# A graph layer that sorts its edges on the chip: three parts and eight rounds become five parts and ten rounds

## The chip, the core and the metric

The kernel runs on one core of a Trainium2 chip. TensorE (PE; its weight loads are listed as PEld), VectorE (DVE), ScalarE (ACT) and GpSimd (POOL) work side by side, each through its own list of instructions in order; SyncE (SP) here only issues DMAs. The metric is the device time of one execution in microseconds, lower is better. Three runs of the kernel before took 4861.4 to 4865.1 us, median 4864.8.

## What is computed

There are 12,500 nodes with 128 features, and 412,500 edges with 64 features, given in the order of `dst`. The reference, cut to what matters:

```python
h = x @ Wn + bn; q = x @ Wq + bq; k = x @ Wk + bk; v = x @ Wv + bv
eh = edge_attr @ We + be
hmid   = leaky_relu(concat([q[src], k[dst], eh], -1) @ A1 + b1, 0.2)
scores = leaky_relu(hmid @ A2 + b2, 0.2)
w   = softmax(scores.mean(-1), axis=0)              # over all edges
out = segment_sum(w[:, None] * v[dst], src)
y   = layernorm(h + out) * gamma + beta
result = layernorm(x + y)
```

So each edge needs rows of `k` and `v` by `dst`, in whose order the edges stand, and a row of `q` by `src`, in which they are random; and its weighted `v` is added up by `src`.

## The kernel before

*Making records.* The 412,500 edges are 403 groups of 1024. The nodes are split by `src` into 98 blocks of 128. For a group, PE gathers the rows of `k` and `v` with one-hot matrices and adds the edge features (L931, L936); ACT copies the 128 x 260 records out of PSUM (L946); DVE works out where each record belongs, namely the next free place of its block (`onehots`, `masked`, `places`: L851 to L913); POOL writes them there with eight indirect DMAs of 128 records a group (`evacuate`, L958). The place is in a table `rtab` in DRAM, in which each block has `cap` rows. `make(p)` does this for the groups of a part p. It yields six times a group, and between the yields the program puts other work.

*Parts and tables.* `PARTS` cuts the 403 groups into three parts that end at groups 165, 307 and 403. There are two tables (`TABS = 2`), and part p writes to table p % 2. In a block the records of a part fill tiles of 128 rows: `tiles` is how many a part can need (the mean and 4.4 standard deviations), 15, 13 and 9 here, 37 together. The largest sets `cap`.

*Rounds.* A part's tiles are read back in rounds, before the part has ended where that is certain: round r covers tiles t0 to t0 + t of every block, and may begin at a group at which these tiles are full in all blocks (the mean less 4.4 standard deviations); the last round of a part waits for the part's end. The eight rounds have 5, 4, 6 tiles a block, 4, 4, 5, and 4, 5. A *unit* is up to three blocks of a round and at most 15 tiles (`WIDTH`, `BLK`): 33 units in most rounds, 49 in the round of six tiles, 280 together.

*A unit's work* (functions inside `sums_of`): `load` (SP, L1150) brings the tiles, `load_q` the blocks' rows of q. `sources` takes the block-local node numbers, `turn` and `turned` transpose them (PE, ACT), `put` writes them to DRAM from ACT's queue and `spread` (SP, L1204) reads them back onto all partitions. For each slice of four tiles `onehot` (DVE, L1216; one instruction for each block that the slice touches), `hidden` (PE), `sloped` (ACT), `leaky` (DVE, L1253); then `scores`, `above_zero`, `heads`, and for a running softmax `maxima`, `maximum`, `reference` (L1320), `weights`; for each slice `select` (DVE, L1338), `weigh` (ACT, L1352), `add` (PE, L1381); at last `total` (DVE, one L1397 for each block, with the sums of the round before, which `before_it` loaded) and `store`.

*The order.* Everything is put in order by hand. `sums_of` gives each of these functions a step; units follow one another at `every` = 8 steps, 6 or 8 in the last round, and `lags` says how many steps each function stands before or after the unit's own. The last loop of `sorted_path` lays the steps of round r beside the groups from `begun[r]` to `begun[r + 1]`. `begun` is worked out beforehand: a round begins when its tiles are certain and the round before is through, and one that has T tiles in U units is taken to last (T + 2.7 U)/12 groups (`PACE`). Before, the rounds begin at groups 74, 127, 167.1, 227.1, 278, 318.1, 367 and 407.1. What is left when the groups are made is done after them, then the last round with more buffers, then the closing (`closing`): the two norms and the output.

*Fills.* Rows of a block that may stay empty in the first two parts must hold zeros. `fill_piece` (L572) writes them with DMAs on SP: 49 for the first table up to group 72, 49 from `zeros` in DRAM for the second table between groups 74 and 163.

*Checks on the chip.* `certain`, `ended` and `gated` compare the counts of the records with the bounds that the plan assumed; `ended` also makes the mask that the last round of a part uses to leave out rows that no record has reached. In each, `counted` copies the counts (PSUM) to SBUF first.

*Order of DMAs.* A load must come after the scatters whose rows it reads. Where a scatter and a load touch the same table but never the same rows, `declare_no_dep` says so; what isn't declared is waited for.

## Time and profile before

| | before |
|---|---|
| median of 3 runs | 4864.8 us |
| the profiled execution | 4862.1 us |
| its span, first to last instruction | 4860.4 us |
| mean granted TensorE clock | 0.927 |
| busy PE, DVE, ACT, POOL | 4017.1 (83%), 4104.8 (84%), 3110.9 (64%), 3305.1 (68%) us |
| DMA | 1484 MB, mean 305 GB/s |
| first and last scatter begin | 59.0, 4310.6 us |

The profile cuts the span into 40 slices of 121.5 us. Rows of the slices hold one digit for each, the busy share in tenths. In the groups of instructions stand line, engine, operation, what is written and read, shape and count; after the bar the busy time in us and the mean duration of one in ns; after the second bar the idle time just ahead of them and what ended it. A group's busy time counts overlapping instructions once, so it can be less than count times mean. The rows of stretches of time are explained where they stand.

### The profile page before, as it was taken

The page shows a single profiled execution, that of the slowest core. Times are in us where ns is not written, and L with a number is a line of the kernel's source. Part 1 is how long each engine was busy: PE and PEld are TensorE (multiplying, and loading weights), DVE is VectorE, ACT ScalarE, POOL GpSimd, SP SyncE. Part 2 cuts the span into 40 slices and gives each one's busy share as a digit, 9 for nine tenths or more (in the row PEclk, how much of TensorE's full clock was granted, in tenths as well). Part 3 has the DMA queues.
Part 4 walks back from the last instruction along what each step waited for, and adds up shares of the span by engine and source line. Part 5 has one row for each costly group of instructions (what it writes and reads, how often), then busy time and mean ns, then how long its engine had stood idle before and what let it go on. Part 6 is the DMA issues. An engine that isn't in the chain of part 4 may idle for free. (4 is left out here: it accounts for less than half of the span.)

```text
span 4860.4 us, 84339 instructions
## 1 busy us (share of the span) xinstructions
PE 4017.1 (83%) x26346; PEld 3094.3 (64%) x26626; DVE 4104.8 (84%) x8629; ACT 3110.9 (64%) x8211; POOL 3305.1 (68%) x3280
## 2 busy tenths in 40 slices
PE   3655665688888899999998888899899999998997
PEld 2434443566766666777676666666677777666776
DVE  8878886698888888889898888898999998977877
ACT  2332222477776667777776666676777777777886
POOL 4777777777777767777777777777777777731103
PEclk7777776799999999999999999999999999999999
DMA  6778876999999998999998888999999999989964
GB/s 197 265 252 266 269 266 214 335 358 346 350 338 346 363 337 307 310 321 313 322 313 311 301 295 301 322 338 321 329 337 329 340 322 322 339 286 329 324 222 162
DMA packets 608627, 1484.42 MB, mean 305 GB/s; under 512 B 101632, under 2 KB 309395, under 8 KB 606374
## 3 DMA queue, kind: packets, MB, share of 16 engines
q1 hardware_dynamic: 445822, 1049.05, 64.5%
q0 software_dynamic: 154752, 429.39, 23.2%
q8 instruction: 211, 3.46, 0.3%
q14 instruction: 250, 2.05, 0.1%
q10 hardware_dynamic: 7592, 0.48, 0.1%
HBM read 906.61 MB, written 611.06 MB: 312 GB/s over the span
## 5 line engine op out<-in xcount | busy, mean ns | idle before, releaser
L958 POOL DMA_INDIRECT rtab<-rec,idx x3224 | 3220.9, 999 | 1087.4 <-issue 775.9
L946 ACT ACTIVATE rec<-pkv 128x1024 f32<-128x1024 f32 x806 | 821.7, 1019 | 1090.4 <-DMA rtab<-rec,idx 557.5
L1352 ACT ACTIVATE ohw<-ohs,w 128x128 f32<-128x128 bf16 x3626 | 1187.0, 399 | 70.8 <-DVE ohs L1338 39.0
L1381 PE MATMUL psm<-rt,ohw 128*128 128x128 f32 x7252 | 1020.6, 284 | 3.0 <-ACT ohw L1352 2.5
L1381 PEld LDWEIGHTS psm<-rt,ohw 128*128 128x128 f32 x7252 | 934.6, 196 | 82.2 <-ACT ohw L1352 21.4
L936 PE MATMUL pkv<-WeS,eat 128*128 128x256 f32 x3224 | 932.3, 416 | 0.0
L1253 DVE TENSOR_TENSOR hm<-ph,hm 128x512 f32<-128x512 f32 (+1 forms) x932 | 625.0, 671 | 294.9 <-ACT hm L1249 292.8
L931 PE MATMUL pkv<-kvs,ohd 128*128 128x256 bf16 x3224 | 534.5, 293 | 325.9 <-ACT rec L946 319.6
L931 PEld LDWEIGHTS <-ohd 128*128 128x128 bf16 x3224 | 319.4, 105 | 581.0 <-issue 461.9
L936 PEld LDWEIGHTS pkv<-WeS,eat 128*128 128x128 f32 x3224 | 612.5, 211 | 72.2
L1230 PE MATMUL ph<-ident,rt 128*128 128x128 f32 x3626 | 581.3, 282 | 76.8 <-DVE hm L1253 74.8
L1230 PEld LDWEIGHTS ph<-ident,rt 128*128 128x128 f32 x3626 | 415.2, 145 | 304.5 <-issue 145.5
L1216 DVE TENSOR_SCALAR ohT<-rowB,iotaP,power 128x512 bf16<-128x512 uint8 (+3 forms) x1176 | 577.2, 509 | 30.1 <-DMA rowB<-row 30.0
L1249 ACT ACTIVATE hm<-ph 128x512 f32<-128x512 f32 (+1 forms) x932 | 532.6, 571 | 61.8 <-PE ph L1239 25.4
L872 DVE TENSOR_SCALAR ohd<-dstb,node 128x1152 bf16<-128x1152 uint8 x404 | 565.0, 1399 | 6.1 <-PE pkv L931 6.1
L1239 PE MATMUL ph<-ohT,qs 128*128 128x512 bf16 (+2 forms) x2072 | 495.3, 329 | 41.1 <-DVE ohT L1216 24.0
L900 DVE TENSOR_TENSOR ats<-pc,oh 128x792 f32<-128x792 f32 x403 | 392.0, 973 | 27.5 <-PE pc L880 27.5
L1264 PE MATMUL psc<-hm,A2s 128*32 128x512 f32 (+2 forms) x1864 | 370.1, 607 | 44.7 <-DVE hm L1253 33.7
L862 DVE TENSOR_REDUCE few<-oh 128x99 bf16<-128x792 bf16 x403 | 395.1, 980 | 13.9
L1338 DVE TENSOR_TENSOR ohs<-iotaE,sl 128x512 bf16<-128x512 bf16 (+1 forms) x932 | 395.2, 424 | 5.0 <-ACT ohw L1352 4.8
L911 DVE TENSOR_REDUCE pos<-ats 128x8 f32<-128x792 f32 x403 | 390.5, 969 | 1.9
L1329 ACT ACTIVATE w<-S,ref 128x12 f32<-128x12 f32 (+2 forms) x280 | 84.7, 302 | 340.6 <-DVE ref L1320 327.7
(193 smaller groups left out, 4072.3 us busy)
## 6 DMA issues: line engine op xcount, KB each, us to landing
rt<-rtab SPq DMA_DIRECT2D x177, 1560.0 KB
rt<-rtab SPq DMA_DIRECT2D x96, 1950.0 KB
eat<-in_ea SPq DMA_DIRECT2D x201, 512.0 KB
rtab<-rec,idx POOLq DMA_INDIRECT x3224
dstb<-dtab SPq DMA_DIRECT2D x201, 256.0 KB
qs<-qtab SPq DMA_DIRECT2D x224, 192.0 KB
atab<-old SPq DMA_DIRECT2D x224, 192.0 KB
rtab<-zeros SPq DMA_DIRECT2D x49, 780.0 KB
```

What stands on the lines that cost most here:

```text
L872: nc.vector.tensor_scalar(to, row[:, cols], node, None, op0=ALU.is_equal)
L931: nc.tensor.matmul(pk[:, i, h, :], ohd[t], kvs, start=(h == 0), stop=False,)
L936: nc.tensor.matmul(pk[:, i, :, :D], eat[:, (j + i) * P : (j + i + 1) * P], WeS, start=False, stop=True,)
L946: nc.scalar.activation(rec[:, :, :, : 2 * D], pk, AF.Copy)
L958: one_tile = nc.gpsimd.indirect_dma_start(out=rtab[p % TABS][:, :], out_offset=bass.IndirectOffsetOnAxis(ap=idxs[g][:, t : t + 1], axis=0) ...
L1216: nc.vector.tensor_scalar(st["oh"][k][:, (a - t0) * P : (b - t0) * P], st["rowB"][:, a * P : b * P], iotaP, power[:, bs[u] : bs[u] + 1], o ...
L1230: nc.tensor.matmul(ph[:, j * P : (j + 1) * P], st["rt"][:, t0 + j, :D], ident, is_transpose=True, start=(j == 0), stop=False,)
L1239: nc.tensor.matmul(ph[:, cols], st["qs"][:, j0 // t, s, :], oh[:, cols], start=False, stop=(s == 1 and j1 == t0 + n),)
L1249: nc.scalar.activation(hm, state[i]["ph", k][:, : n * P], AF.Copy, scale=SLOPE)
L1253: nc.vector.tensor_tensor(hm, ph[:, : n * P], hm, op=ALU.max)
L1352: nc.scalar.activation(ohw[:, j, :], ohs[:, :, j], AF.Copy, scale=st["w"][:, t0 + j : t0 + j + 1])
L1381: nc.tensor.matmul(st["psS"][:, (1 + u) * P : (2 + u) * P], ohw[:, j, :], st["rt"][:, t0 + j, D : 2 * D], start=(k == 0), stop=(k == t - 1),)
```

## The change

The parts and rounds, the pace that the plan assumes, and what follows from them:

- Five parts end at groups 142, 227, 323, 363 and 403. Their blocks need 13, 8, 9, 4 and 4 tiles, 38 together. Ten rounds of 5, 3, 5 | 3, 5 | 3, 2, 4 | 4 | 4 tiles a block, of 33 units each: 330 units.
- The plan takes a round to last (T + 1.2 U)/11.2 groups. The rounds begin at groups 74, 121.3, 151.1, 198.4, 228.1, 275.4, 305.2, 326.2, 364.8 and 403.3.
- The first, third and fifth part share the first table. The fifth part's records stand nine tiles up in each block (`ABOVE`), above the third's nine tiles. So it may write while the third is still read, and that is declared. `cap` becomes 13 tiles.
- Two mask buffers in place of one. The counts are compared where they are, in PSUM, without the copy.
- A unit of two slices gets the lags of one of three.
- The 49 fills of the second table lie between groups 10 and 134.

```diff
-PARTS = (74, 127, 165), (225, 278, 307), (367, 403)
+PARTS = (74, 113, 142), (189, 227), (274, 301, 323), (363,), (403,)
+ABOVE = (0, 0, 0, 0, 9)
-PACE = 12
+PACE = 11.2
...
-        most = max(self.tiles)
+        most = max(t + above for t, above in zip(self.tiles, ABOVE))
...
-    maskp = pool("mask", 1)
+    maskp = pool("mask", 2)
...
+                    if ABOVE[p]:
+                        for k in range(len(PARTS[p - TABS])):
+                            tc.declare_no_dep(
+                                one_tile, group=f"loads{p - TABS}.{k}", reason="other tiles"
+                            )
...
-            runf = counted()
-            pcs.pop(p)
+            run = pcs.pop(p)
             low, over = lims.pop(p)
-            worst(low, runf, low, 2 + 2 * r)
-            worst(runf, over, over, 3 + 2 * r)
+            worst(low, run, low, 2 + 2 * r)
+            worst(run, over, over, 3 + 2 * r)
...
-            o = lags(p, nk)
+            o = lags(p, max(nk, 3))
...
+            t0 += ABOVE[p]
...
+            if p + TABS < NP and ABOVE[p + TABS]:
+                for k in range(len(PARTS[p + TABS])):
+                    tc.declare_no_dep(rows_in, group=f"rows{p + TABS}.{k}", reason="other tiles")
...
-        free_at += sum(len(bs) * t + 2.7 for q, bs, _ in units if q == p) / PACE
+        free_at += sum(len(bs) * t + 1.2 for q, bs, _ in units if q == p) / PACE
...
-            1, n1, n2 - 12, zeros
+            1, 60, n2 - 48, zeros
...
-        fills = fills[::-1]
+        fills = sorted(fills, key=lambda piece: piece[0])[::-1]
```

20 lines of the change are left out of this document (10 added, 10 removed).

## The prediction

> **What bounds the kernel now.** First the page's slices, to see which resource is full and where.
>
> ```profile
> DMA  6778876999999998999998888999999999989964
> GB/s 197 265 252 266 269 266 214 335 358 346 350 338 346 363 337 307 310 321 313 322 313 311 301 295 301 322 338 321 329 337 329 340 322 322 339 286 329 324 222 162
> q0 software_dynamic: 154752, 429.39, 23.2%
> ```
>
> Then the scatter's own line, and the loads that read the table back, each with its first and last start:
>
> ```profile
> L958 POOL DMA_INDIRECT rtab<-rec,idx x3224: 954/960/2788, 59.0 to 4310.6; - x190
> L1150 SPq DMA_DIRECT2D rt<-rtab x280: 370/416/1373, 864.9 to 4672.1; - x140
> ```
>
> So there are three stages: making alone until 864, making and reading together until 4311, and a tail of 549.4 us to the end of the span. Last, the busy times by stretch (length, then PE, PEld, DVE, ACT and POOL busy with instructions, clock, DMA share, GB/s). The windows of the rounds reach from a round's first running reference (L1320) to its last: rounds 0, 1, 4, 5; then the busiest slice, the whole middle stage, and the tail up to round 7 and through it.
>
> ```profile
> 927.00:1449.00 522.00, 456.71 (x3283) 366.84 (x3311) 467.37 (x944) 382.37 (x1001) 398.38 (x405) 0.98 1.00 349
> 1462.00:1901.00 439.00, 390.27 (x2547) 295.79 (x2578) 369.44 (x780) 298.04 (x827) 315.46 (x320) 0.95 0.96 338
> 3056.00:3483.00 427.00, 387.79 (x2578) 293.66 (x2608) 374.59 (x788) 299.36 (x831) 323.68 (x330) 0.97 0.93 326
> 3502.00:3981.00 479.00, 437.61 (x3180) 355.74 (x3209) 451.62 (x970) 380.85 (x1013) 367.06 (x368) 0.97 0.95 333
> 3767.00:3889.00 122.00, 113.22 (x829) 92.52 (x836) 116.63 (x249) 96.95 (x258) 93.66 (x94) 0.97 0.97 341
> 864.00:4311.00 3447.00, 3070.60 (x20919) 2375.40 (x21162) 3035.19 (x6313) 2432.60 (x6608) 2599.51 (x2632) 0.97 0.94 328
> 4311.00:4398.00 87.00, 76.03 (x499) 54.63 (x506) 55.09 (x152) 54.66 (x169) 4.74 (x3) 0.95 0.86 299
> 4398.00:4717.00 319.00, 295.31 (x2345) 238.35 (x2373) 251.61 (x680) 279.82 (x823) 25.12 (x12) 1.00 0.84 288
> ```
>
> Eight scatters are one group. Round 0: 405 scatters, 50.6 groups, 10.31 us a group; round 1: 40 groups, **10.98**; round 4: 41.25, 10.35; round 5: 46, 10.41. POOL issues at nearly the same pace although DVE's share goes from 0.84 (round 1) to 0.94 (round 5), so the middle stage goes at POOL's pace, about 10.35. Only round 1 is slower; there the fills of the second table share the DMA engines. In the busiest slice POOL still does 94 scatters, with DVE at 116.63/122 = 0.956. The tail has no POOL work: PE is busy 295.31 of 319.
>
> The profiled execution took 4862.1 us (span 4860.4 and 1.7 around it); the median of the runs shown, 4864.8, lies 2.7 above. The sum is made against 4862.
>
> **The change, part by part.** Its plan follows from the sizes (412,500 edges, 98 blocks, 403 groups). Before, eight rounds of 5, 4, 6 | 4, 4, 5 | 4, 5 tiles a block. After, ten of 5, 3, 5 | 3, 5 | 3, 2, 4 | 4 | 4: 38 tiles, and 33 units in each round, 330 in place of 280.
>
> *Tail.* Before, the last round had 15 tiles a unit; now it has 12. Before it was to begin at 407.1 groups, 4.1 after the last, so 4.1/40.1 of round 6's 264 steps, 27 steps or 3.4 units, were left: at 319/32 = 9.97 us a unit, 33 us of the 87. After, 403.3: two steps, 2 us. So 87 becomes 56. A unit of 15 keeps PE busy 295.31/32 = 9.23 us. What doesn't shrink with tiles is mainly the sum over heads, eight instructions of 72.8/576 = 0.126:
>
> ```profile
> L1290 PE MATMUL psm<-headsum,z 128*128 128x4 f32 x576 | 72.8, 244 | 18.8 <-ACT ohw L1352 6.1 <-DVE old L1397 4.2 <-ACT rec L946 2.7
> ```
>
> The other 8.2 over 15 tiles gives 6.6 for 12, with the heads 7.6; at PE's share of 0.926 that is 8.2 us a unit. That is the low end, 9.97 (nothing shrinks) the high one. I take 8.7, near the low end, because the turn and the maximum don't shrink either. 32 × 8.7 = 278, and from 4717 to the end of the span, 143, stays: 56 + 278 + 143 = 477, **72 saved** (88 to 31).
>
> *Middle stage.* The work taken out of the tail, and one more tile a block, must fit beside the same 329 groups. Units a group rise: 33 over 29.8 groups is 1.107 with 3 tiles (three rounds), 33/21 = 1.571 with 2, 33/38.5 = 0.857 with 4 (two rounds), 33/47.3 = 0.698 with 5 (three rounds). DVE's prices (groups of DVE's instructions, in 3524 to 3889; the last two rows are of the whole run):
>
> ```profile
> L872 DVE TENSOR_SCALAR ohd<-dstb,node 128x1152 bf16<-128x1152 uint8 x35 | 49.1, 1403 | 0.0
> L900 DVE TENSOR_TENSOR ats<-pc,oh 128x792 f32<-128x792 f32 x36 | 35.0, 972 | 0.5 <-PE pc L880 0.5
> L911 DVE TENSOR_REDUCE pos<-ats 128x8 f32<-128x792 f32 x36 | 34.8, 968 | 0.1
> L862 DVE TENSOR_REDUCE few<-oh 128x99 bf16<-128x792 bf16 x35 | 34.3, 981 | 1.2
> L851 DVE TENSOR_TENSOR oh<-blk,iotaE 128x792 bf16<-128x792 bf16 x35 | 19.7, 562 | 0.0
> L913 DVE SCALAR_TENSOR_TENSOR idx<-pos,twin 128x8 int32<-128x8 f32 x36 | 6.0, 167 | 1.2
> L1253 DVE TENSOR_TENSOR hm<-ph,hm 128x512 f32<-128x512 f32 x73 | 49.7, 681 | 8.8 <-ACT hm L1249 8.7
> L1253 DVE TENSOR_TENSOR hm<-ph,hm 128x384 f32<-128x384 f32 x24 | 13.2, 552 | 3.7 <-ACT hm L1249 3.7
> L1216 DVE TENSOR_SCALAR ohT<-rowB,iotaP,power 128x512 bf16<-128x512 uint8 x25 | 14.0, 559 | 0.1
> L1216 DVE TENSOR_SCALAR ohT<-rowB,iotaP,power 128x384 bf16<-128x384 uint8 x48 | 23.5, 490 | 0.0
> L1216 DVE TENSOR_SCALAR ohT<-rowB,iotaP,power 128x256 bf16<-128x256 uint8 x48 | 19.2, 442 | 0.0
> L1216 DVE TENSOR_SCALAR ohT<-rowB,iotaP,power 128x128 bf16<-128x128 uint8 x24 | 8.4, 348 | 0.0
> L1338 DVE TENSOR_TENSOR ohs<-iotaE,sl 128x512 bf16<-128x512 bf16 x72 | 29.8, 415 | 0.0
> L1338 DVE TENSOR_TENSOR ohs<-iotaE,sl 128x384 bf16<-128x384 bf16 x24 | 10.5, 438 | 0.0
> L1397 DVE SCALAR_TENSOR_TENSOR old<-old,by,psm 128x128 f32<-128x128 f32 x72 | 20.5, 339 | 1.5 <-PE psm L1381 1.5
> L1319 DVE TENSOR_REDUCE m<-psm 128x1 f32<-128x128 f32 x24 | 6.8, 282 | 0.0
> L1305 DVE TENSOR_REDUCE mx<-S 128x1 f32<-128x15 f32 x24 | 4.1, 169 | 0.8
> L1253 DVE TENSOR_TENSOR hm<-ph,hm 128x256 f32<-128x256 f32 x3 | 1.2, 417 | 0.0
> L1338 DVE TENSOR_TENSOR ohs<-iotaE,sl 128x256 bf16<-128x256 bf16 x3 | 0.9, 286 | 0.0
> ```
>
> A group: 1.403 + 0.972 + 0.968 + 0.981 + 0.562 + 0.167 = 5.05. Whatever its tiles, a unit has three `old` (1.02), `m` (0.28) and four short ones such as `mx` (0.67): 1.97. Slices hold four tiles, and L1216 splits a slice at each block. 5 tiles: hm 2.60, ohT 2.77, ohs 1.68, in all 9.02. 4 tiles: 2.04, 1.68, 1.25, in all 6.93. 3 tiles, slices of 4, 4 and 1: hm 1.64, ohT 0.490 + 0.348 + 2 × 0.442 + 0.348 = 2.07, ohs 1.03, in all 6.71 (the 128-wide hm and ohs are not in the trace: 0.28 and 0.2 by the steps between the widths). 2 tiles: 1.10, 1.33, 0.70, in all 5.10. A unit of nine tiles costs DVE nearly what one of twelve does. Durations overlap: round 5 adds up to 32.5 × 9.02 + 46 × 5.05 = 525 against 451.62 busy, and round 4 to 434 against 374.59: 0.86 of the sum. Busy DVE a group after:
>
> - 5 tiles 0.86 × (0.698 × 9.02 + 5.05) = 9.76; 4 tiles 9.45; **3 tiles 10.73; 2 tiles 11.23**.
>
> The first two lie under POOL's pace, the last two above it. How full DVE can get isn't shown: at least 0.956, where POOL hadn't slowed, at most 1. I take 0.98: 10.95 and 11.46 us a group.
>
> Sum by planned groups (98 blocks of t tiles and 1.2 for each of 33 units, over 11.2; together 329): round 0, 47.3 × 10.33 = 489 (round 0's pace); two rounds of 5, 94.6 × 10.41 = 985 (round 5's); three of 3, 89.4 × 10.95 = 979; the one of 2, 21 × 11.46 = 241; two of 4, 77 × 10.35 = 797 (round 4's): 3491. At the end of a part PE begins the next counts only when DVE has read the old ones (the one wait of this kind in 1560 to 1860):
>
> ```profile
> PEld pc L800 <- DVE run L995: 3.7, 1, 3.7
> ```
>
> Two more ends, 3 us each: 3497, that is **50 more** than 3447. With DVE at 1 it is 25 less, at 0.956 30 more. PE's share, 3070.60/3447 = 0.89 now, rises too; up to the tail's 0.926 I count no stall of its own.
>
> Short slices pay more than their share: from 512 to 256 columns `hm` falls by 264 ns, from 681 to 417, so some 153 ns are left at no columns. [...]
>
> *Fills.* The second table's 49 moves leave groups 74 to 163 and go to 10 to 134. Until 74 they meet DMA shares of 0.6 to 0.8, as the page's row shows: nothing, up to 10 if SP's queue is held. What round 1 lost (10.98 against 10.41, over 40 groups 23 us) isn't in my sum, so this gain is counted.
>
> *Latency in the round of 2.* Steps per unit stay at eight, while a unit takes only 11.46 × 21/33 = 7.3 us. In eight steps the numbers of a unit go from ACT to DRAM and back to all partitions; SP waits for the first half alone:
>
> ```profile
> SPq L1204 <- DMA row<-slT: 1918.3, 277, 13.0
> ```
>
> 1918.3/277 = 6.9 us. Behind it on SP stand the loads of `old`, `rt`, `qs`, `kvs` and `eat`, all needed later. If the trip needs a tail unit's 9.97 us, 33 units lose 88 us; at best nothing. I take nothing, since DVE has other units' work ahead of it, and keep 88 for the range.
>
> *The rest* is nothing: the counts read from PSUM without a copy save some ten DVE instructions of 99 columns; the second mask buffer costs memory alone, and lets a mask be made while the one before is read; the fifth part's place above the third's lets scatters go on while round 7 still reads, as the pauses at part ends need.
>
> Sum: 4862 + 50 − 72 = **4840**.
>
> **Rivals.** (a) *POOL keeps its pace* everywhere: DVE overlaps more, and 329 × 10.35 = 3405, or up to 3462. Time 4748 to 4805. For it: no slowing at 0.956. Against it: 10.73 and 11.23 of pure DVE work.
>
> (b) *Gain and loss cancel*: the middle grows by 62 to 82, 4852 to 4872.
>
> (c) *Slower: the DMA engines become the bound.*
>
> ```profile
> rt<-rtab SPq DMA_DIRECT2D x177, 1560.0 KB
> eat<-in_ea SPq DMA_DIRECT2D x201, 512.0 KB
> dstb<-dtab SPq DMA_DIRECT2D x201, 256.0 KB
> kvs<-kvtab SPq DMA_DIRECT2D x403, 64.0 KB
> qs<-qtab SPq DMA_DIRECT2D x224, 192.0 KB
> ```
>
> A group moves 256 + 128 + 64 and eight scatters of 130 (429.39 MB/3224): 1488 KB. A unit moves 130 a tile, three times 192 and 16 a tile: 2766, 2328, 1890, 1452 KB for 5, 4, 3, 2 tiles. Round 4 checks: 139 MB in 427 us, 326 GB/s. After, the stage moves 1193 MB in place of 328 × 3.447 = 1131. Break-even is 1193/(3447 + 72) = 339 GB/s: round 0 held 349 at full pace, round 1 lost pace at 338. If all 329 groups go at round 1's 10.98, the stage takes 3612, and the time is 4862 + 165 − 72 = 4955.
>
> (d) *The tail doesn't shrink with its tiles*, being bound by its chain (9.97): 31 saved, 4881; or the row trip of round 6 costs its 88: 4928.
>
> (e) *The short instructions' latency doesn't overlap.* Without the 0.86, 3 tiles take 12.5 us a group and 2 tiles 13.1; those rounds alone add 171: 5011. Against it: round 5 would take 525/46 = 11.4 and took 10.41. [...]
>
> **How the numbers follow.** Chances: forecast (4805 to 4852) 0.36; (a) 0.18; (b) 0.14; (c) 0.24; (d) 0.07; (e) 0.01. About 0.2% is what a measurement can tell from no change. Faster 0.54, same 0.14, slower 0.32. The range leaves out the best half of (a) and the worst of (c): 4775 to 4915; the forecast's own is 4805 to 4852.
>
> **What would show it.** Right: the last scatter near 4361 and 477 from there to the end, units of the last round 8.7 us apart, 10.9 us a group in the rounds of 3 with DVE over 0.96. Wrong: a last scatter at 4311 or before (a), or past 4400 with DVE waiting for `rt` or `rowB` (c, d); last units still 10 us apart (d).

## The result and the profile after

| | before | after |
|---|---|---|
| median of 4 runs | 4863.7 us | 5182.2 us |
| lowest and highest | 4861.4, 4865.1 | 5174.9, 5196.9 |
| the profiled execution, its span | 4862.1, 4860.4 us | 5181.2, 5179.4 us |
| busy DVE | 4104.8 us (84%) | 4310.3 us (83%) |
| last scatter begins, first rows loaded | 4310.6, 864.9 us | 4712.5, 873.1 us |

The changed kernel takes 1.0659 times as long, with a 95% interval of 1.0635 to 1.0683. That is 6.6% slower, and outside the predicted range of 4775 to 4915. First the lines of the scatters and of the loads of the changed kernel: kind and count, shortest, median and longest duration in ns, first and last start.

```profile
L963 POOL DMA_INDIRECT rtab<-rec,idx x3224: 954/960/2823, 59.3 to 4712.5; - x190
L1155 SPq DMA_DIRECT2D rt<-rtab x330: 370/408/1491, 873.1 to 4995.9; - x165
```

The first stage ends 8 us later than before. The middle stage, from the first load to the last scatter, takes 3840 us in place of 3447, **393 more** (predicted: 50). The tail takes 5179.4 - 4712.5 = 467 us in place of 549, **82 less** (predicted: 72). So the whole miss lies in the middle.

Next the busy times by stretch of the changed kernel, with the columns of the same view of the kernel before: stretch and length, then PE, PEld, DVE, ACT and POOL busy with instructions, clock, DMA share, GB/s. The first nine are rounds 0 to 8 from their first reference (L1328) to their last, round 8 cut at the last scatter; then the rest of round 8, round 9, and the middle stage.

```profile
938.00:1413.00 475.00, 434.49 (x3201) 349.10 (x3201) 435.43 (x903) 367.01 (x976) 352.17 (x359) 0.98 0.98 343
1425.00:1814.00 389.00, 331.93 (x2283) 256.25 (x2281) 325.33 (x796) 260.10 (x732) 243.07 (x245) 0.96 0.87 291
1833.00:2305.00 472.00, 430.75 (x3167) 346.53 (x3168) 436.97 (x957) 374.01 (x1003) 347.29 (x351) 0.98 0.93 325
2317.00:2708.00 391.00, 334.27 (x2281) 258.27 (x2281) 326.08 (x798) 259.81 (x733) 243.92 (x246) 0.95 0.85 284
2725.00:3197.00 472.00, 430.59 (x3162) 349.16 (x3164) 438.61 (x956) 373.81 (x1002) 344.42 (x351) 0.97 0.94 326
3209.00:3583.00 374.00, 326.22 (x2224) 253.10 (x2223) 309.61 (x776) 250.82 (x716) 221.47 (x223) 0.95 0.85 276
3592.00:3920.00 328.00, 282.00 (x1665) 204.28 (x1664) 239.93 (x619) 205.20 (x571) 177.70 (x181) 0.90 0.79 258
3932.00:4347.00 415.00, 381.70 (x2554) 286.44 (x2553) 363.95 (x772) 293.76 (x822) 293.92 (x301) 0.98 0.92 319
4360.00:4713.00 353.00, 322.85 (x2200) 244.79 (x2199) 307.48 (x661) 253.76 (x715) 253.74 (x258) 0.99 0.92 319
4713.00:4768.00 55.00, 48.56 (x304) 33.06 (x303) 31.97 (x87) 33.02 (x103) 2.56 (x2) 0.94 0.81 288
4768.00:5041.00 273.00, 266.35 (x1840) 196.59 (x1838) 200.19 (x530) 212.71 (x664) 27.89 (x13) 0.99 0.83 292
873.00:4713.00 3840.00, 3411.82 (x23575) 2649.14 (x23575) 3317.27 (x7501) 2725.56 (x7479) 2596.57 (x2631) 0.96 0.90 309
```

A round has 33 units, and so 32 intervals between its first and last reference; POOL's count over eight gives its groups. That makes this table (DVE's share is its busy time over the length):

| round, tiles | us between units | groups between units | us a group | DVE's share | predicted us a group |
|---|---|---|---|---|---|
| 0, 5 tiles | 14.84 | 1.40 | 10.58 | 0.92 | 10.33 |
| 2 and 4, 5 tiles | 14.75 | 1.37 | 10.76 | 0.93 | 10.41 |
| 7, 4 tiles | 12.97 | 1.18 | 11.03 | 0.88 | 10.35 |
| 1 and 3, 3 tiles | 12.16, 12.22 | 0.96 | 12.70, 12.72 | 0.84, 0.83 | 10.95 |
| 5, 3 tiles | 11.69 | 0.87 | 13.42 | 0.83 | 10.95 |
| 6, 2 tiles | 10.25 | 0.71 | 14.50 | 0.73 | 11.46 |

Two things stand out. In the rounds of three and two tiles, which were to be bound by DVE at 0.98, DVE is busy 0.84 to 0.73 of the time, and no other column is full in its place: PE is at 0.85 to 0.87, and the DMA share falls to 0.87 to 0.79. And a unit doesn't get shorter in proportion to its tiles. From 15 tiles and 1.37 groups to 6 tiles and 0.71 groups it goes from 14.75 to 10.25 us. A straight line through these two is 5.5 us for a unit and 6.8 us for a group beside it; the rounds between lie within 0.5 us of that line (0.96 groups: 12.0 by the line, 12.2 measured).

The line describes these rounds; it can't tell what a unit costs by itself, because tiles and groups fall together in it. Two things on record hold one of them fixed. In the run with the plan's old pace (`e1_old_pace`, below) the rounds of three and two have the same tiles and 0.05 to 0.09 groups more to a unit; summed over the four rounds, a unit takes 0.81 us more for 0.27 groups, some 3 us a group. By that a unit of nine tiles has about 9 us of its own (12.2 less 0.96 groups at 3), an estimate from single runs. And units of the last round, which has an order of its own and no groups, take 8.5 us with 12 tiles here and took 10.0 with 15 before. So the part that doesn't shrink with the tiles, called the toll below, is large, but its size isn't settled. More rounds of fewer tiles are more units, and every unit pays it.

Where the 343 us beyond the forecast lie: the rounds of three and two tiles took 1482 us for 895 scatters, 111.9 groups; at the predicted 10.95 and 11.46 they would have taken 1237, so **245** are theirs. The rounds of five and four took 2187 us for 202.5 groups, 2100 by the forecast: **87**. The other 11 are in the turns from round to round.

Last the waits, first in a round of three tiles after (2317 to 2708), then in a round of four before (3056 to 3483, 427 us): who waited for whom, us in total, times, longest (`issue`: idle time for which the profile shows no cause).

```profile
ACT w L1337 <- DVE ref L1328: 70.6, 28, 5.2
POOL rtab L963 <- issue: 56.9, 186, 0.6
DVE hm L1261 <- ACT hm L1257: 56.0, 36, 3.4
POOL rtab L963 <- ACT rec L952: 46.1, 23, 4.9
```

```profile
ACT w L1329 <- DVE ref L1320: 50.6, 23, 4.5
ACT rec L946 <- PE pkv L936: 45.4, 17, 4.7
DVE hm L1253 <- ACT hm L1249: 32.4, 30, 3.6
ACT rec L946 <- DMA rtab<-rec,idx: 12.7, 8, 3.8
```

Before, ACT at times waited for the DMAs of scatters before it wrote records (12.7 us); POOL's side was the later one. After, it is POOL that waits for ACT's records (46.1 us). DVE's whole idle time in this round is 391 - 326 = 65 us, and 56 of them are one wait: the leaky maximum (L1261) for ACT's slopes (L1257), 1.7 us a unit. ACT in its turn stands 70.6 us, 2.2 us a unit, before the weights (L1337), for the reference (L1328), which DVE makes once PE has turned the maxima. Slopes and records stand behind the weights in ACT's list, and they can be late with them: ACT stood idle for 5.16 us and began the weights at 2461.13; the slopes behind them began at 2463.83, and at 2464.32 the copy of records whose product (L941) PE had ended at 2459.10.

### The profile page after: what moved, and what is told of

Same layout as the page of the kernel before. It is cut to its first block, busy times and chain, and to the rows that moved or that the text cites. A ratio compares the mean times of both kernels' runs of the same rounds, so it can differ in the third digit from the quotient of the medians.

```text
span 5179.4 us, 90440 instructions
## 1 busy us (share of the span) xinstructions
PE 4299.8 (83%) x28288; PEld 3302.9 (64%) x28288; DVE 4310.3 (83%) x9597; ACT 3312.5 (64%) x8854; POOL 3309.2 (64%) x3280
## 5 line engine op out<-in xcount | busy, mean ns | idle before, releaser
L951 ACT ACTIVATE rec<-pkv 128x1024 f32<-128x1024 f32 x806 | 821.3, 1019 | 1053.7 <-PE pkv L941 514.1
L1360 ACT ACTIVATE ohw<-ohs,w 128x128 f32<-128x128 bf16 x3724 | 1228.7, 399 | 79.6 <-DVE ohs L1346 32.8
L1389 PE MATMUL psm<-rt,ohw 128*128 128x128 f32 x7448 | 1082.9, 287 | 11.3 <-ACT ohw L1360 10.3
L1389 PEld LDWEIGHTS psm<-rt,ohw 128*128 128x128 f32 x7448 | 977.7, 196 | 105.4 <-ACT ohw L1360 33.5
L1261 DVE TENSOR_TENSOR hm<-ph,hm 128x512 f32<-128x512 f32 (+3 forms) x1046 | 655.7, 627 | 403.3 <-ACT hm L1257 401.8
L941 PE MATMUL pkv<-WeS,eat 128*128 128x256 f32 x3224 | 941.8, 420 | 0.0
L936 PE MATMUL pkv<-kvs,ohd 128*128 128x256 bf16 x3224 | 541.4, 296 | 289.8 <-ACT rec L951 285.6
L1238 PE MATMUL ph<-ident,rt 128*128 128x128 f32 x3724 | 614.8, 283 | 88.5 <-DVE hm L1261 87.2
L1224 DVE TENSOR_SCALAR ohT<-rowB,iotaP,power 128x256 bf16<-128x256 uint8 (+3 forms) x1469 | 657.1, 472 | 36.7 <-DMA rowB<-row 36.5
L941 PEld LDWEIGHTS pkv<-WeS,eat 128*128 128x128 f32 x3224 | 618.5, 213 | 74.5
L936 PEld LDWEIGHTS <-ohd 128*128 128x128 bf16 x3224 | 317.9, 105 | 526.5 <-issue 416.7
L1247 PE MATMUL ph<-ohT,qs 128*128 128x256 bf16 (+3 forms) x2938 | 586.8, 304 | 43.7 <-DVE ohT L1224 43.4
L1238 PEld LDWEIGHTS ph<-ident,rt 128*128 128x128 f32 x3724 | 426.2, 145 | 295.0 <-issue 129.2
L1257 ACT ACTIVATE hm<-ph 128x512 f32<-128x512 f32 (+3 forms) x1046 | 561.2, 537 | 64.0 <-PE ph L1247 22.6
L877 DVE TENSOR_SCALAR ohd<-dstb,node 128x1152 bf16<-128x1152 uint8 x404 | 565.0, 1399 | 6.1 <-PE pkv L936 6.1
L1272 PE MATMUL psc<-hm,A2s 128*32 128x512 f32 (+3 forms) x2092 | 440.4, 587 | 47.4 <-DVE hm L1261 41.0
L1346 DVE TENSOR_TENSOR ohs<-iotaE,sl 128x512 bf16<-128x512 bf16 (+3 forms) x1046 | 436.0, 417 | 0.8 <-ACT ohw L1360 0.8
L1337 ACT ACTIVATE w<-S,ref 128x15 f32<-128x15 f32 (+3 forms) x330 | 99.8, 302 | 526.2 <-DVE ref L1328 516.8
L867 DVE TENSOR_REDUCE few<-oh 128x99 bf16<-128x792 bf16 x403 | 395.1, 980 | 13.9
```

Source lines behind the costliest of these rows:

```text
L877: nc.vector.tensor_scalar(to, row[:, cols], node, None, op0=ALU.is_equal)
L936: nc.tensor.matmul(pk[:, i, h, :], ohd[t], kvs, start=(h == 0), stop=False,)
L941: nc.tensor.matmul(pk[:, i, :, :D], eat[:, (j + i) * P : (j + i + 1) * P], WeS, start=False, stop=True,)
L951: nc.scalar.activation(rec[:, :, :, : 2 * D], pk, AF.Copy)
L1224: nc.vector.tensor_scalar(st["oh"][k][:, (a - t0) * P : (b - t0) * P], st["rowB"][:, a * P : b * P], iotaP, power[:, bs[u] : bs[u] + 1], o ...
L1238: nc.tensor.matmul(ph[:, j * P : (j + 1) * P], st["rt"][:, t0 + j, :D], ident, is_transpose=True, start=(j == 0), stop=False,)
```

## The experiments

Two readings were tested first. *The unit's toll is DVE's*: DVE's own work and its waits in series set the pace. *It is something else*: PE, whose share was 0.85 to 0.92 in the rounds, the DMA engines, the plan's tighter pace, or the fills. Each experiment was executed once, unless an interval is given; the four runs of the changed kernel spread over 22 us, so smaller differences say nothing. The kernel before, run beside them, took 4854 to 4872 us. The changed kernel's 5181.2 us is what the differences are taken from.

### The plan's pace, the fills, and the width of units

The old pace in the changed kernel (`e1_old_pace`):

```diff
-PACE = 11.2
+PACE = 12
-        free_at += sum(len(bs) * t + 1.2 for q, bs, _ in units if q == p) / PACE
+        free_at += sum(len(bs) * t + 2.7 for q, bs, _ in units if q == p) / PACE
```

> The changed kernel with the plan's old pace ((T + 2.7 U)/12 groups a round): rounds of 3 lie over 31.9 groups instead of 29.8, of 2 over 23.8 instead of 21, and 13 units of round 8 are left when the groups are made. Theory W (a unit costs VectorE its work and its waits wherever it lies): the middle stage loses 13 units, the tail gains them; 5170 to 5240 in all. Rival O (the rounds are only pressed too tight, and spread out they go at POOL's pace again): last scatter 4330 to 4420, 4870 to 4980 in all.

Measured: 5165.9 us, 15 less, no more than the spread, and just below the 5170 to 5240 of the first case. The last scatter came 133 us sooner (4579.7), and the tail took 117 us more: what the middle gained by taking fewer units came back in the tail, so the plan isn't pressed too tight; the work is too long.

The new place of the fills alone, in the kernel before (`e5_before_fills`):

```diff
-            1, n1, n2 - 12, zeros
+            1, 60, n2 - 48, zeros
-        fills = fills[::-1]
+        fills = sorted(fills, key=lambda piece: piece[0])[::-1]
```

> The kernel before with the new place of the second table's fills alone (groups 10 to 163 in this plan instead of 74 to 163). The prediction's step: round 1 goes at 10.4 instead of 10.98 us a group, 15 to 23 us less: 4840 to 4850. Rival (the fills cost the first stage as much as they cost round 1): 4855 to 4870.

Measured: 4856.8 us, ratio 0.9994 (0.9981 to 1.0008). The move does nothing that can be seen. It isn't the round without fills, though: in this plan the fills reach to group 157, so 7 of them still begin in round 1, where 15 did; that round took 437 us in place of 439.

Smaller units in the kernel before: with a width of 12, its rounds of five tiles have 49 units of ten tiles in place of 33 of fifteen (`e13_before_width12`). Parts, tables, fills and pace stay.

```diff
-WIDTH = 15
+WIDTH = 12
-    TM = max(min(BLK, WIDTH // t) * t for *_, t in plan.rounds)
+    TM = 15
```

> The kernel before with units of at most 12 tiles: rounds 0, 5 and 7 (5 tiles a block) get 49 units of ten tiles instead of 33 of fifteen; nothing else. Theory W (each unit has its own waits and fixed work): rounds 0 and 5 rise from 10.33 and 10.45 to 11 to 12 us a group, 5000 to 5080 in all. Theory B (only VectorE's busy time counts, up to a share of 0.98): its work is 9.4 to 9.8 us a group, under POOL's pace; only the tail's 16 more units count: 4870 to 4910.

Measured: 5098.1 us, 5% slower. Its rounds 0 and 5 by stretch:

```profile
909.00:1513.00 604.00, 531.37 (x3557) 405.42 (x3603) 497.37 (x1093) 416.20 (x1126) 424.46 (x432) 0.96 0.94 319
3553.00:4148.00 595.00, 524.50 (x3527) 401.81 (x3574) 495.71 (x1129) 424.88 (x1166) 407.43 (x414) 0.97 0.85 288
```

48 intervals: 12.6 and 12.4 us a unit, 11.2 and 11.5 us a group, with DVE at 0.82 and 0.83. In the kernel before, the same tiles in units of fifteen went at 10.3 and 10.4. The tiles, the edges and the DMA bytes (1484 MB) are the same; only the number of units rose. So the toll isn't a matter of the new parts. Of the 236 us, 135 had come by the last scatter (4445.4 in place of 4310.6); the other 101 are the tail, whose last round has 16 units more.

### What one wait is worth

Without the reference in the weights, in the changed kernel and in the one before (`e3_no_ref`, `e6_before_no_ref`). The running maximum is still computed, but the exponentials take a constant instead of it.

```diff
-                st["w"][:, :nt], st.pop("S")[:, :nt], AF.Exp, bias=ref[:, u : u + 1],
-                scale=1.0 / H,
+                st["w"][:, :nt], st.pop("S")[:, :nt], AF.Exp, bias=eps,
+                scale=1e-6,
```

> The changed kernel with the weights of a unit taken without the running reference (the exponential gets a constant bias and a scale of 1e-6): what is left out is that each unit's weights are relative to the maximum so far, so ScalarE no longer waits for VectorE's reference (516.8 us of waits in the changed kernel); every instruction stays. Theory A (a unit costs some 6 us of the interleaved program whatever its tiles, because ScalarE, in order, stands still until the chain maximum, TensorE, reference is through, and the record copies and the slopes behind it come late): units of the rounds of 3 come 10 to 11 us apart instead of 12.2, those of 2 under 9.5 instead of 10.3, the last scatter 200 to 350 us earlier, 4850 to 4980 us in all. Theory B (VectorE's own work is the limit, only at a share of 0.83 and not 0.98): the waits move elsewhere, 5140 to 5190.

> The kernel before with the same part left out (the weights' reference). Both theories: its middle stage goes at POOL's pace, so at most the slow stretches go (to 329 x 10.35 = 3405, 42 us) and a little of the tail: 4800 to 4865.

Measured: 5059.7 us, 122 less; in the kernel before 4838.6, 22 less than its neighbour. The first lies between its two cases, the second in the range that was expected. The round of three and the round of two of the changed kernel without the reference:

```profile
2292.00:2658.00 366.00, 323.51 (x2292) 257.93 (x2290) 325.19 (x800) 260.95 (x736) 244.78 (x246) 0.96 0.90 304
3510.00:3813.00 303.00, 265.75 (x1653) 197.38 (x1653) 241.80 (x624) 204.75 (x573) 174.28 (x180) 0.92 0.85 281
```

The round of three goes from 391 to 366 us with the same 325 us of DVE work, so DVE's share rises to 0.89. The last scatter came 125 us sooner, so all of it is the middle's. The wait for the reference is part of the toll, a third of what the middle lost, and no more.

The leaky maximum one step later (`e11_leaky_later`), so that ACT has more time for the slopes:

```diff
-        f = L + 4 + 3 * e
+        f = L + 5 + 3 * e
-            leaky=2, scores=L + 1, above=L + 2 + e, heads=L + 3 + 2 * e, maxima=f,
+            leaky=3, scores=L + 2, above=L + 3 + e, heads=L + 4 + 2 * e, maxima=f,
```

> The changed kernel with VectorE's part of the slope (leaky) one step later in the order of every round but the last, and all behind it one step later too. Theory W (VectorE's in-order stream is the loop: its own work and, in each unit, 1.75 to 2.5 us in which it stands still for ScalarE's slope, so short rounds pay that more often per group): most of the 401.8 us of these waits go, units of the rounds of 3 come 10.8 to 11.4 us apart instead of 12.2, 4950 to 5080 in all. Rival (the waits only show where the engines' chains meet; another wait takes their place): 5150 to 5220.

Measured: 5180.1 us, no change. Rows of the waits over the whole run, of the changed kernel and then of this one:

```profile
ACT w L1337 <- DVE ref L1328: 516.8, 253, 6.9
...
DVE hm L1261 <- ACT hm L1257: 401.8, 329, 3.6
...
POOL rtab L963 <- ACT rec L952: 241.1, 141, 5.0
```

```profile
ACT hm L1257 <- PE ph L1247: 489.4, 281, 6.1
...
POOL rtab L963 <- ACT rec L952: 311.1, 158, 5.6
...
DVE hm L1261 <- ACT hm L1257: 151.2, 139, 3.5
...
ACT w L1337 <- DVE ref L1328: 98.8, 79, 3.3
```

The move did what it was to do: DVE's wait for the slopes fell to 151 us, and ACT's for the reference to 99. But ACT now waits 489 us for PE's hidden layer (L1247), 22.6 in the changed kernel. The rival was right for the total: a wait that is moved turned up on the next engine. By rounds it was not nothing: the second round of three took 371 us in place of 391, but the round of two 340 in place of 328, and the first of four 425 in place of 415.

The weights and all behind them two steps later, for units of up to three slices (`e16_weights_later`, and the same in the kernel before, `e17_before_weights_later`):

```diff
+        x = 2 if nk <= 3 else 0
-            reference=f + 2 + e, weights=f + 3 + e, old=f - 1, lowered=f + 6 + e,
+            reference=f + 2 + e, weights=f + 3 + e + x, old=f - 1, lowered=f + 6 + e + x,
...
```

> The changed kernel with a unit's weights, and what follows from them, two steps later in the order, for units of up to three slices outside the last round; the result is the same. If ScalarE's wait for the reference holds up the slopes and copies behind it (leaving the reference out gave 122 us), most of that comes without leaving anything out: 5040 to 5090. Rival (as with the later slope, another wait takes its place): 5150 to 5200.

> The kernel before with the same move. Its middle stage goes at POOL's pace in most rounds; leaving the reference out gave 22 us there. If the wait is what counts: 4835 to 4852. Rival: 4855 to 4870.

Measured: 5119.2 us, 62 less, half of what leaving the reference out gave and short of the 5040 to 5090 expected; in the kernel before 4887.5, ratio 1.0034 (1.0021 to 1.0048), slightly slower, and above both of its cases.

### What each engine's work is worth

Work was added to DVE (the count of the one-hots, L867, twice) and to ACT (the first copy of the records, L951, twice), in every group, and work was left out: the sums of the second and third block of a unit on DVE (L1405), one of the two products of q on PE (L1247).

```diff
+                nc.vector.tensor_reduce(
+                    few[g], oh.rearrange("p h b t -> p b h t"), AX.XY, ALU.add
+                )
```

```diff
+            if j == 0:
+                nc.scalar.activation(rec[:, :, :, : 2 * D], pk, AF.Copy)
```

```diff
-            for u in range(m):
+            for u in range(1):
```

```diff
-                for s in range(2):
+                for s in range(1):
```

> The changed kernel with one more VectorE instruction per group: the count L867 (0.98 us) done twice with the same result. Theory B: in the rounds of 3, 2 and 4 tiles (about 190 groups) each group takes 0.9 us more, and those of 5 a little: 5330 to 5400. Theory A: VectorE stands idle for 17% there, most of it goes into the idle time: 5190 to 5260.

> The changed kernel with one more ScalarE instruction per group: the first of the two record copies L951 (1.02 us) done twice with the same result. Theory A: ScalarE's order is the loop, so the rounds of 3, 2 and 4 tiles take 0.9 us more a group: 5330 to 5400. Theory B: ScalarE is busy for only 66% there, so nothing comes of it: 5180 to 5220.

> The changed kernel with one instead of up to three L1405 per unit: the other blocks of a unit keep the sums of the round before, their new sums are left out. VectorE has 0.5 to 0.7 us less to do per unit, at the end of a unit's chain. If VectorE's stream is the bound of the short rounds, a unit comes 0.5 to 0.7 us sooner (rounds of 3: 11.5 to 11.7 instead of 12.2), 5000 to 5070 in all. If the bound is TensorE's stream: 5140 to 5185.

> The changed kernel with one instead of two products of the one-hot rows with q (L1247): the lower half of q's bits is left out. TensorE has some 0.8 us less to do per unit (in the rounds of 3 L1247 is busy 52.4 us for 32 units). If TensorE's stream is the bound: 4950 to 5030. If VectorE's is: 5130 to 5185.

Measured, in this order: 5521.5, 5275.9, 5112.3 and 5212.3 us. 0.98 us more for DVE in each of 329 groups are 322 us, and cost 340: the full price and a little more, above both cases. (The expectation of `e18` below spread this cost over all 403 groups, hence its 0.84 a group.) 1.02 us more for ACT are 336 and cost 95, between the cases. DVE's two sums of 0.34 us less in 297 units are 202 us; DVE's busy time in the middle fell by 124 (3317.27 to 3193.64), less than that in part because durations overlap (all 882 such sums of the changed kernel, 341 ns each, add up to 301 us and keep DVE busy for 252.6), and 69 came back, again between the cases. PE's product less gave nothing: the time is 31 us longer, more than the spread, though PE was busy 90 us less in the middle (3411.82 to 3322.10); the granted clock of the run was 0.903 in place of 0.920. The round of three with the doubled count, then with the sums left out:

```profile
2434.00:2860.00 426.00, 351.26 (x2280) 270.54 (x2280) 357.96 (x832) 260.94 (x733) 246.38 (x249) 0.90 0.81 263
```

```profile
2302.00:2681.00 379.00, 331.47 (x2274) 260.92 (x2274) 309.55 (x731) 259.93 (x732) 243.12 (x244) 0.95 0.88 290
```

35 us longer than 391, for 31 counts that keep DVE busy 32 us more. DVE's idle time stays: 426 - 358 = 68 us, 65 before. Work and waits stand in series on DVE, so its stream is on the path though DVE isn't full. Two reservations: the granted clock fell from 0.95 to 0.90 in this round, and PE was busy 17 us longer with the same work; and the count is one that PE's sums wait for (L885: 98.4 us in 40 waits in the changed kernel), so another DVE instruction need not cost as much. Taking work away gives back less: 69 of 124 us. So something close behind takes over.

To measure this from the other side, two thirds of the one-hot columns of dst were left out (L877; the records then hold the rows of k and v of wrong nodes), in the changed kernel and in the one before, and combined with the earlier edits (`e18` to `e21`). Two last ones leave the product of the edge features out of the records (L941), alone and with both others (`e22`, `e23`).

```diff
-            for r in (slice(0, 3),) if g + 1 < G or first else (slice(0, 2), slice(2, 3)):
+            for r in (slice(0, 1),):
...
-                wide[:, t // 3, t % 3 * P : t % 3 * P + P] for t in range(first, first + GT)
+                wide[:, 0, t % 3 * P : t % 3 * P + P] for t in range(first, first + GT)
```

```diff
-                        start=(h == 0), stop=False,
+                        start=(h == 0), stop=(h == 1),
...
-            for i in range(2):
-                nc.tensor.matmul(
-                    pk[:, i, :, :D], eat[:, (j + i) * P : (j + i + 1) * P], WeS,
-                    start=False, stop=True,
-                )
```

> The changed kernel with a third of the one-hot columns of dst made for each group (384 of 1152; the rows of k and v of the other tiles come from wrong nodes). DVE's instruction goes from about 1.40 to about 0.5 us, 0.9 us a group less. It is the mirror of the doubled count (0.98 us more cost 0.84 us a group). If DVE's own stream, work and waits in series, sets the pace of the changed kernel, 0.84/0.98 of it is saved in 329 groups: about 250 us, 4900 to 4960, and a unit of 3 tiles takes about 11.4 us. If DVE and the other engines bind each other, so that less work on DVE only lengthens its waits, a third is saved, as with the sums left out: 70 to 110 us, 5070 to 5115.

> The kernel before with the same part left out. If its making and reading goes at a pace set elsewhere than on DVE, as the prediction read it, the time stays within 30 us: 4830 to 4870. If DVE's stream sets the pace there too, 0.75 us a group less, about 250 us: 4600 to 4660.

> The changed kernel with both left out: two thirds of the dst one-hot columns, and the reference in the weights (which alone took 122 us off). If DVE's work and its waits stand in series, the savings add up: about 370 us, 4780 to 4850. If one of them binds only while the other is there, the time is little below the lower of the two alone: 4880 to 4940 when the first alone gives 4930, 5020 to 5060 when it gives 5090.

> The changed kernel without the reference in the weights and with the leaky maximum one step later. Without the reference DVE still waited 196 us for ACT's slopes. If that wait is now what the time hangs on, moving it takes most of it away: 4880 to 4960. If the units' chain only shifts its waits, as it did with the leaky maximum moved alone, the time stays at 5040 to 5070.

> The changed kernel with the product of the edge features left out of the records (eight matmuls a group; they kept PE busy 67.0 us in the round of 391 us, 2.2 us a group). If PE's stream sets the pace, up to POOL's 10.4 us a group is reached: 4790 to 4900. If DVE's stream, work and waits in series, sets it, PE being in front of it only in short waits: 5120 to 5190. If the engines bind each other, a part of the 2.2 us a group comes back: 4920 to 5110, and DVE's share in the rounds of three rises from 0.83.

> The changed kernel with three parts left out: edge features in the records, the reference in the weights, two thirds of the dst one-hot columns (the last two alone gave 4963). If what was left in the rounds of three and two tiles (11.4 and 13.4 us a group, PE at 0.91 and 0.89) was PE, they come to 10.4 to 10.8 and 11.5 to 12 and the time to 4830 to 4890. If it was a chain of steps that no engine's work lengthens, they stay: 4930 to 4965.

| left out of the changed kernel | us | against 5181.2 |
|---|---|---|
| dst columns (`e18`) | 5040.1 | -141 |
| reference in the weights (`e3`) | 5059.7 | -122 |
| both (`e20`) | 4962.8 | -218 |
| reference; leaky later (`e21`) | 5137.3 | -44 |
| edge product (`e22`) | 5126.0 | -55 |
| edge product, reference, dst columns (`e23`) | 4885.9 | -295 |

Against what was expected: `e18` and `e20` lie between their cases, `e21` above both of its cases, `e22` in the range for DVE's stream. The time of `e23` lies in the range that was set for PE as the bound (4830 to 4890), though its rounds of three and two are slower than that case had them.

The kernel before without the dst columns (`e19`) took 4834.8 us, 34 less than beside it. DVE's instruction fell from 1403 to 410 ns (the expectation's 0.5 us was a little high), so 327 us of DVE work went: the changed kernel gives back 0.43 of it, the one before 0.1. (DVE's busy time in the middle of the changed kernel fell by 307 us, to 3010.22; 141 are 0.46 of that, and the 69 of 124 were 0.56.) Two rounds of the kernel before without the columns (its rounds 4 and 5, of four and five tiles):

```profile
3040.00:3451.00 411.00, 382.52 (x2597) 290.82 (x2596) 336.27 (x784) 297.64 (x828) 314.68 (x317) 0.98 0.96 334
3470.00:3956.00 486.00, 443.91 (x3211) 359.05 (x3210) 409.73 (x969) 381.47 (x1015) 372.71 (x372) 0.97 0.94 329
```

411/39.6 = 10.4 and 486/46.5 = 10.5 us a group, as with all the DVE work (10.35 and 10.41), with DVE's share down to 0.82 and 0.84. That is a floor which doesn't depend on DVE's work. Nor is it the DMA engines, whose share is 0.96 and 0.94 here: round 3 of the kernel before, of four tiles with 1.48 groups to a unit, goes at 489/47.5 = 10.3 as well, with DVE at 0.84, PE at 0.85 and a DMA share of 0.87:

```profile
2553.00:3042.00 489.00, 413.75 (x2711) 314.43 (x2742) 410.99 (x832) 315.96 (x862) 373.49 (x380) 0.96 0.87 303
```

The changed kernel reaches the floor too once it is relieved. A round of three, the round of two and a round of five, without dst columns (`e18`), then without the reference as well (`e20`), then without the edge product too (`e23`):

```profile
2259.00:2632.00 373.00, 334.19 (x2281) 261.71 (x2281) 295.80 (x798) 259.88 (x734) 245.68 (x249) 0.95 0.90 300
3476.00:3793.00 317.00, 278.05 (x1668) 205.29 (x1667) 220.06 (x623) 204.82 (x571) 176.28 (x180) 0.91 0.82 267
2648.00:3097.00 449.00, 420.96 (x3173) 343.77 (x3173) 398.02 (x960) 373.48 (x1004) 343.86 (x346) 1.00 0.96 341
```

```profile
2244.00:2600.00 356.00, 324.56 (x2279) 256.42 (x2279) 295.76 (x796) 259.03 (x734) 248.42 (x250) 0.96 0.93 315
3422.00:3720.00 298.00, 264.01 (x1658) 196.90 (x1655) 218.43 (x620) 204.00 (x574) 175.62 (x179) 0.93 0.86 284
2615.00:3064.00 449.00, 421.46 (x3170) 344.75 (x3170) 398.01 (x956) 372.27 (x1005) 343.53 (x347) 0.99 0.97 340
```

```profile
2224.00:2569.00 345.00, 287.15 (x2044) 219.00 (x2044) 294.86 (x797) 259.54 (x734) 246.52 (x249) 0.92 0.95 324
3384.00:3671.00 287.00, 234.60 (x1480) 165.83 (x1479) 219.14 (x624) 204.53 (x575) 174.94 (x179) 0.90 0.90 298
2584.00:3035.00 451.00, 375.86 (x2781) 299.40 (x2811) 397.66 (x957) 371.69 (x1004) 344.99 (x348) 0.95 0.96 341
```

The round of five takes 449, 449 and 451 us: 10.4 us a group in all three. It is at the floor after the first relief, and nothing more helps it. The round of three goes 391, 373, 356, 345, and the round of two 328, 317, 298, 287: each relief takes a part, and with all three they are at 11.1 and 12.8 us a group, still above the floor, with DVE at 0.85 and 0.76 and PE at 0.83 and 0.82. No engine is full there; the DMA share, 0.95 and 0.90, is high again, but the round of five goes at the floor with 0.96. DVE's idle time in the round of three shows the same from inside: 65 us at first, 77 without the columns (30 us of work gone, 18 of them gained), 60 without the reference as well.

What follows. In the rounds of five the middle goes close to POOL's pace, and at it without the dst columns; they are at the edge, since the doubled count costs its price there too (`e7`: 518 us in place of 472 in round 2). In those of three and two, and of four where less than 1.2 groups lie beside a unit, it goes at the pace of the unit: a round of steps through DVE, PE and ACT, in which every engine waits a little for another (in the round of three DVE 56.0 us for ACT's slopes, ACT 70.6 for DVE's reference, PE 24.8 for DVE's maxima, L1313). Work on DVE lies on it in full when added; less DVE work, one wait less, or less PE work shortens it by a part, and the savings nearly add (141 and 122 give 218, with 55 more 295 of 318). PE alone is not the bound: without the edge product it was busy 344 us less in the middle (3411.82 to 3067.54), and 55 came back. The 2.2 us a group that the product had taken would be 724 us; not all of it was gained: the other matmuls took longer, at a lower granted clock (last section). With DVE relieved the same product gives 77 (`e20` to `e23`), so PE's work counts for a part there. That the steps' waits make up the rest of the toll is argued, not shown: the reference is the one wait that was taken out. Where the last 1 to 2 us a group of these rounds come from is open. Moving steps was tried only in three ways, and one of them (`e21`) lost 78 of the 122 us that leaving out the reference had gained, most of it in the rounds of two and four (round of two: 334 us, and 303 without the reference alone). The number of steps to a unit (`every`) wasn't changed, and making the slopes on another engine wasn't tried.

None of these runs keeps all of the computation and is clearly faster than the kernel before; the two that only move something in it (`e5`, `e17`) gave 0.9994 and 1.0034 of its time.

## Why the prediction was wrong

- **What bounds the kernel before: right, for what it said.** POOL's pace of about 10.35 stands when 327 us of DVE work are taken away (`e19`: 10.4 and 10.5). But it was read from rounds with 1.2 to 1.6 groups a unit, and the forecast used it at 0.7 to 1.4. (Round 0's pace was read as 10.31 and used as 10.33: 1 us.)
- **Tail, 72 saved: right.** 82 were. The rest of the round before last took 55 us (56 predicted), the last units came 273/32 = 8.5 us apart (8.7), and 138 us remained (143). The first half of rival (d), a tail that doesn't shrink, falls with it.
- **DVE's work a group: right.** 10.73 was forecast for three tiles, and 326.08/30.75 = 10.6 were busy; 11.23 for two, and 239.93/22.6 = 10.6, because 1.41 units came to a group in place of 1.57; 9.76 for five, and 436.97/43.9 = 10.0; 9.45 for four, and 363.95/37.6 = 9.7. One single price was off. The short slices of `ohs`, put at 0.2 us by the steps between the widths, take 0.437, longer than the wide ones; those of `hm`, put at 0.28, take that. These are the groups of DVE's instructions in the round of three, with count, busy time and mean of one in ns:

```profile
L1346 DVE TENSOR_TENSOR ohs<-iotaE,sl 128x512 bf16<-128x512 bf16 x64 | 26.6, 416 | 0.0
L1346 DVE TENSOR_TENSOR ohs<-iotaE,sl 128x128 bf16<-128x128 bf16 x32 | 14.0, 437 | 0.0
L1261 DVE TENSOR_TENSOR hm<-ph,hm 128x128 f32<-128x128 f32 x30 | 8.5, 282 | 0.3 <-ACT hm L1257 0.3
```

- **The step that failed: "How full DVE can get isn't shown: at least 0.956, where POOL hadn't slowed, at most 1. I take 0.98".** It was 0.83 in the rounds of three and 0.73 in the round of two. The 0.956 came from 122 us of a round in which 1.4 groups of work lay beside each unit; the forecast took it for a property of DVE. A share that is reached with much other work between a unit's steps says nothing of units that come closer together. The sign of this was on the page: ACT's wait for the reference and DVE's wait for the slopes were there before, and cost little (`e6`: 22 us without the reference). The rows of the waits of the kernel before:

```profile
ACT w L1329 <- DVE ref L1320: 327.7, 178, 5.2
DVE hm L1253 <- ACT hm L1249: 292.8, 285, 5.0
```

  With 330 units in place of 280, and less beside each, they grew to 516.8 and 401.8 us, and cost more (`e3`: 122).
- **Rounds of four and five at their old pace of 10.33 to 10.41: wrong by the same step.** They took 10.6 to 11.0, 87 us together. Beside 32 units stood 37.6 groups in the round of four, where the kernel before had 40 and 41.3, and 43.9 to 44.9 in the rounds of five, where it had 50.6 and 46. With fewer groups to a unit, these rounds came out of POOL's cover as well.
- **Latency in the round of two, taken at nothing: wrong in size, by another cause.** Its units came 10.25 us apart, not 7.3; 32 x 2.95 = 94 us, near the 88 kept for the range. But it wasn't the trip through DRAM: over the whole run DVE waited 36.5 us for `rowB`, in this round 0.8, while 79.9 of its 88 idle us there were the wait for ACT's slopes.
- **Fills, 23 us counted: not borne out.** The move alone gives 0.9994 of the time (0.9981 to 1.0008), and round 1 took 437 us in place of 439 with less than half of its fills left in it.
- **Rivals.** (c), 4955 by the DMA engines, is refuted: the middle moved 309 GB/s, below the 339 of its break-even, and in the slow rounds 258 to 291 at shares of 0.79 to 0.87. The sign that it named, DVE waiting for `rt` or `rowB`, didn't come: 77 and 36.5 us in the whole run. (a) and (b) fall with the middle. (e), a latency of short instructions (some 153 ns, estimated from two rows of `hm`) that doesn't overlap, gave 5011, the nearest, and its 12.5 us a group for three tiles is close to the 12.7 found, but by the wrong mechanism: the durations in the round of three add up to 381 us, against 326 busy, so they overlap as before (0.86). None of the rivals was a stall between engines without a full one; the two that spoke of waits, (d) and the latency step, put them in the row's trip.

## What to carry to other kernels

A unit that passes through several engines, each with its list in order, need not get shorter in proportion to what is in it: here units of 15 to 6 tiles came 14.75 to 10.25 us apart, and the same tiles in more units of ten cost the kernel before 5% (`e13`). Here cutting work into more units was paid for as soon as the other stream no longer covered it. With 1.29 groups beside a unit of 12 tiles the kernel before kept 10.35 us a group, and the changed one took 11.0 with 1.18; with 15 tiles it was 10.4 at 1.44 groups, and 10.8 at 1.37. So before costing an edit by the busy time of the fullest engine, put the time between units against what is in them and beside them, for all rounds of the trace, and look at the waits between engines that are hidden now.

## What the runs showed of the hardware

TensorE's granted clock was lower in two runs that left PE idle more (`e22` and `e7`). In the round of three it was 0.95 in the changed kernel, and 0.87 without the edge product, though that round took only 3 us less:

```profile
2289.00:2677.00 388.00, 311.69 (x2024) 232.76 (x2026) 325.67 (x795) 259.12 (x732) 244.03 (x246) 0.87 0.86 286
```

PE's share went from 334.27/391 = 0.85 to 311.69/388 = 0.80. The eight matmuls a group that are gone had kept PE busy 67.0 us of this round, but its busy time fell by 22.6. Over the whole run the mean clock was 0.920 and 0.856 (the kernel before, executed beside the second, had 0.933), and the matmuls that stayed took longer: those of the sums (L1389) 299 ns in place of 287, those of the identity (L1238) 294 in place of 283, those that gather `k` and `v` (L936) 317 in place of 296. So a part of the time taken from PE was given back by slower matmuls. The doubled count of `e7`, which left PE's work as it was and stretched the round, went the same way: 0.90 in its round of three, at a PE share of 351.26/426 = 0.82. What lowers the clock, and how long PE has to stand idle for it, isn't shown by these runs.

The short one-hot slices were the other surprise: 437 ns for 128 columns against 416 ns for 512. The two write the same kind of tile by the same line, and why the short one isn't shorter was not tried.
